# A graph-network kernel: how many gathered tiles are copied on chip instead, and at which rates

## The chip, the cores and the metric

The kernel runs on one core of one Trainium2 chip. The metric is the time of one execution on the device in microseconds (us). A core has five engines, each with its own instruction stream: TensorE (PE in the profile; its weight loads are PEld), VectorE (DVE), ScalarE (ACT), GpSimd (POOL) and SyncE (SP). They wait for one another through semaphores. Transfers are issued from the queues of SP, ACT and POOL.

## The reference, cut to what matters

One layer of message passing on a graph of 12,500 nodes with 64 features and 200,000 edges sorted by destination, 32 features each. All in float32:

```python
msg_in = concatenate([x[src], x[dst], edge_attr], -1)      # 200000 x 160
messages = relu(msg_in @ mW1 + mb1) @ mW2 + mb2
aggregated = segment_sum(messages, dst, 12500)
u = relu(concatenate([x, aggregated], -1) @ uW1 + ub1) @ uW2 + ub2
out = layernorm(x + u)
```

## The kernel before, in words

The edges are cut into 1563 tiles of 128, and six tiles make a group: 261 groups, number 0 to 260. The kernel first multiplies all nodes with the source part of mW1 (table `tab_a` in memory) and with the destination part (`tab_b`). For each group s it then needs, per edge, the row of `tab_a` that belongs to its source, a window of `tab_b` and the edge features.

There are two ways to the source part.

- **Gathered** (`gather`, L209; L220): one indirect transfer per tile, issued by POOL, brings 128 rows of 128 numbers. A group of which all six tiles are gathered costs six. Gathers run ahead of the rest: `rows` has nine buffers, and a gather waits only for the buffer to come free.
- **Copied** (`singly`, L350, and `joined`, L357): in a copied group the last two of the six tiles are not gathered. Instead x stands transposed on chip (`xtop` with zeros below, `xbot` with zeros above), and for each of 128 pairs of edges one column of `xtop` and one of `xbot` are added into a column of a tile `xc`. ACT makes 64 of these columns (an ACTIVATE with a bias, L355), DVE the other 64 (a bitwise or, L362). The addresses are register values that each engine loads in batches (L331). PE then multiplies `xc` with the source part of mW1 (L387), two more products per copied group, four matrix instructions in the profile.

The main loop goes over the groups. In step s, `node_part(s)` lets DVE add the gathered rows to the products of PE (L410, or L407 over four tiles in a copied group), and ACT takes the relu into `h` (L411, or L408). `collect(s-1)` sums `h` of the group before by destination on PE (L443, and counts in L440). `edge_part(s+1)` makes the products of the next group on PE (L384, L387). Between these stand DVE's share of the copies in two or three parts (`joined`), and after them ACT's share in one piece (`singly`). At 32 points of the list, named in `UPD`, the sums are closed (L457, L458) and the nodes up to there are updated and stored (L480 to L533). The intervals between these points are 49 groups at first, 10 in the middle and 3 to 4 at the end. The tile of products `pc` has two buffers, `h` two, and `xc` three.

Which groups are copied, and when their columns are made, is a list worked out ahead of the run. `PACE` gives a rate of copied groups per step from each step on. `progress(s)` is the sum of the rates up to step s. A group s+3 joins the list `COPIED` whenever the sum passes the next whole number, up to group 257 (`FINAL`). `portion` (L318) gives the columns that step s makes: those between `progress(s-1)` and `progress(s)`, in steps of two columns. So a step makes about 64 times the rate on each of the two engines:

```python
PACE = ((11, 0.42), (50, 0.446), (130, 0.429), (261, 0))
FINAL = 258
def progress(s):
    return sum(r * max(0, min(s + 1, b) - a) for (a, r), (b, _) in zip(PACE, PACE[1:]))
COPIED = []
for s in range(NSUB):
    while progress(s) >= len(COPIED) + 1 and s + 3 < FINAL:
        COPIED.append(s + 3)
```

A step makes 26 to 30 of ACT's columns, 28 in most of them, from step 11 to step 253.

Of the kernel before, what the change touches and what calls it, by code (L numbers as in the profile page):

```python
# [70 lines left out]
U8 = mybir.dt.uint8  # L71
YBASE = XBASE + 4 * XCOLS
LEAD = 8
PACE = ((11, 0.42), (50, 0.446), (130, 0.429), (261, 0))
FINAL = 258


def progress(s):

    return sum(r * max(0, min(s + 1, b) - a) for (a, r), (b, _) in zip(PACE, PACE[1:]))  # L80

# [939 lines left out]
```

## Time and profile before

| what | value |
|---|---|
| median of three runs | 1716.34 us (1715.81 to 1716.83) |
| the profiled execution | 1714.18 us, of which the span from first to last instruction is 1712.3 us |
| PE, busy share | 85%, at a mean granted clock of 0.585 |
| ACT, busy share | 90%; 6720 column copies (L355) take 1274.5 us of it |
| DVE, busy share | 62%; 6720 column copies (L362) take 575.0 us, with 442.2 us of idle time ahead of them |
| POOL, busy share | 75%; 1353 gathers of 944 ns each, 0.30 us apart |

The page lists an engine's busy time with the register loads and waits left out. A group of instructions is given as line, engine, operation, tiles, count, then busy time, the mean duration of one, and the idle time of the engine just before it with what ended that. Instructions of ACT and DVE overlap their successor, so the mean duration is longer than the busy time per instruction.

### The profile page before, as it was taken

How to read it: one execution, taken by the hardware profiler on the slowest of the kernel's cores; microseconds unless marked ns; L12 is line 12 of the kernel's file. 1: busy time of each engine (PE TensorE's matmuls, PEld its weight loads, DVE VectorE, ACT ScalarE, POOL GpSimd, SP SyncE). 2: the span in 40 equal slices, each digit the busy share in tenths (PEclk: the TensorE clock that was granted, in tenths of full speed). 3: DMA queues.
4: the chain of work that ended last, by engine and by line, in shares of the span. 5: the costliest groups of instructions: out<-in, count | busy, mean ns of one | idle time of the engine just before them, and what ended most of it. 6: DMA issues, size and time to landing. Idle time of an engine off the chain costs nothing. (4 is left out here: it accounts for less than half of the span.)

```text
span 1712.3 us, 46949 instructions
## 1 busy us (share of the span) xinstructions
PE 1456.2 (85%) x9604; PEld 1251.9 (73%) x9604; DVE 1053.3 (62%) x7476; ACT 1537.2 (90%) x7151; POOL 1279.5 (75%) x1362
## 2 busy tenths in 40 slices
PE   2696889897888888898889999898878898999998
PEld 2585778776777786887777777776667677777776
DVE  1426666666666666666666666666666666666662
ACT  0277999999999999999999999999999999999982
POOL 7777777777777777777777777777777777777774
PEclk8675555555555555555555555556665656565666
DMA  8783434433333333333334343333333333443342
GB/s 209 207 180 100 119 109 127 117 104 89 98 93 101 95 100 97 99 103 100 104 101 110 106 113 103 106 110 103 106 103 109 111 107 108 113 112 105 105 113 76
DMA packets 205949, 191.23 MB, mean 112 GB/s; under 512 B 56129, under 2 KB 172053, under 8 KB 205669
## 3 DMA queue, kind: packets, MB, share of 16 engines
q1 hardware_dynamic: 147828, 92.48, 19.6%
q0 software_dynamic: 43296, 86.79, 18.6%
q10 hardware_dynamic: 14546, 8.93, 1.9%
q8 instruction: 91, 1.49, 0.4%
q14 instruction: 188, 1.54, 0.3%
HBM read 170.55 MB, written 17.50 MB: 110 GB/s over the span
## 5 line engine op out<-in xcount | busy, mean ns | idle before, releaser
L220 POOL DMA_INDIRECT xg<-tab_a,src_s x1293 | 1221.1, 944 | 394.2 <-issue 357.6
L355 ACT ACTIVATE xc<-xtop,xbot 128x1 f32 x6720 | 1274.5, 288 | 32.9 <-issue 22.9
L362 DVE TENSOR_TENSOR xc<-xtop,xbot 128x1 int32 x6720 | 575.0, 154 | 442.2 <-issue 429.5
L443 PE MATMUL sums<-sel,h 128*128 128x32 f32 x3126 | 643.3, 373 | 83.0 <-ACT h L408 42.5
L443 PEld LDWEIGHTS sums<-sel,h 128*128 128x128 f32 x3126 | 609.5, 296 | 108.0 <-ACT h L408 48.2
L384 PE MATMUL pc<-rhs,l 64*128 64x128 f32 x3126 | 418.7, 413 | 59.3 <-DMA l<-in_eT 15.2
L384 PEld LDWEIGHTS pc<-rhs,l 64*128 64x128 f32 x3126 | 348.8, 293 | 119.4 <-issue 62.8
L410 DVE TENSOR_TENSOR h<-pc,xg 128x768 f32<-128x768 f32 x147 | 139.5, 949 | 57.5 <-PE pc L384 27.8
L411 ACT ACTIVATE h<-h 128x768 f32<-128x768 f32 x147 | 122.3, 833 | 27.6 <-DVE h L410 26.8
L254 DVE TENSOR_TENSOR l<-l,cps 128x768 f32<-128x768 int32 (+1 forms) x134 | 126.7, 946 | 29.3 <-DMA l<-in_dst_row 17.4
L440 PEld LDWEIGHTS <-one 128*1 128x1 bf16 x1563 | 56.9, 83 | 89.3 <-issue 80.3
L440 PE MATMUL cnt<-sel,one 128*1 128x32 bf16 x1563 | 92.6, 187 | 0.5 <-issue 0.3
L408 ACT ACTIVATE h<-pc 128x768 f32<-128x768 f32 x105 | 83.8, 798 | 7.8 <-DVE pc L407 7.4
L407 DVE TENSOR_TENSOR pc<-pc,xg 128x512 f32<-128x512 f32 x105 | 73.4, 699 | 27.9 <-PE pc L387 23.8
L387 PE MATMUL pc<-w1a,xc 64*128 64x128 f32 x420 | 81.2, 388 | 0.0
L260 DVE TENSOR_TENSOR sel<-cps,drc 128x384 f32<-128x384 f32 x131 | 71.4, 545 | 12.0 <-PE sums L443 12.0
L387 PEld LDWEIGHTS pc<-w1a,xc 64*128 64x128 f32 x420 | 72.1, 301 | 0.0
L220 POOL DMA_INDIRECT xg<-in_x,src_s x60 | 57.4, 957 | 19.1 <-issue 17.7
L494 PE MATMUL cps<-ux,xw 128*128 128x64 f32 x252 | 45.9, 341 | 20.0 <-DVE sel L260 17.4
L480 PE MATMUL pu<-xw,uz 128*128 128x480 f32 (+1 forms) x64 | 61.2, 1059 | 0.0
L598 ACT COPY tb<-pb 128x512 f32<-128x512 f32 (+1 forms) x13 | 7.4, 570 | 58.7 <-DMA tab_a<-tb 26.8
L494 PEld LDWEIGHTS cps<-ux,xw 128*128 128x128 f32 x252 | 41.1, 247 | 25.4 <-DVE sel L260 19.6
(105 smaller groups left out, 691.6 us busy)
## 6 DMA issues: line engine op xcount, KB each, us to landing
l<-in_dst_row SPq DMA_DIRECT2D x262, 96.0 KB
l<-in_eT SPq DMA_DIRECT2D x262, 96.0 KB
xg<-tab_a,src_s POOLq DMA_INDIRECT x1293
rhs<-tab_b SPq DMA_DIRECT2D x361, 32.0 KB
tab_b<-tb SPq DMA_DIRECT2D x13, 512.0 KB
rhs<-tab_b SPq DMA_DIRECT2D x387, 16.0 KB
tab_a<-tb ACTq DMA_DIRECT2D x12, 512.0 KB
out<-y SPq DMA_DIRECT2D x31, 128.0 KB
```

Source lines behind the costliest of these rows:

```text
L220: nc.gpsimd.indirect_dma_start(out=a[:, i, :] if s < XG else a[:, i // 2, i % 2, :], out_offset=None, in_=A[:, :] if s >= XG else x[:, :], ...
L254: nc.vector.tensor_tensor(l[r], l[r].bitcast(I32), node[r].unsqueeze(2).broadcast_to([r.stop - r.start, SUP // 2, P]), op=ALU.is_equal)
L355: nc.scalar.activation(o[:, e:e + 1], top.bitcast(F32), AF.Identity, bias=bot.bitcast(F32))
L362: nc.vector.tensor_tensor(o[:, e:e + 1].bitcast(I32), top.bitcast(I32), bot.bitcast(I32), op=ALU.bitwise_or)
L384: nc.tensor.matmul(pc[:, b, k, :], L[g][q:q + 64, m, :], rhs[g % 2][q:q + 64, w, :], start=s >= XG or k == 0, stop=s >= XG and not copied)
L387: nc.tensor.matmul(pc[:, b, k, :], xc[s][q:q + 64], w1a[q:q + 64], start=False, stop=True)
L408: nc.scalar.activation(h, pc, AF.Relu)
L410: nc.vector.tensor_tensor(h[:, b, :m], pc[:, b, :m], a[:, b, :m], op=ALU.add)
L411: nc.scalar.activation(h[:, b, :m], h[:, b, :m], AF.Relu)
L440: nc.tensor.matmul(pn[:, bass.ds(ws[i], WIN)], one, SB[g][:, k0 + i, :, 1], start=False, stop=ends and i == n - 1)
L443: nc.tensor.matmul(ps[:, bass.ds(ws[i], WIN)], h[:, i % 2, i // 2, :], S[g][:, k0 + i, :], start=False, stop=ends and i == n - 1)
L494: nc.tensor.matmul(py[:, i], xw[u % 2][:, i * P:(i + 1) * P], ux, start=i == 0, stop=False)
```

## The change

Only the list is changed: the three rates of `PACE` are higher. The list `COPIED` has 108 groups instead of 105. The first is group 16 as before, the last 257 instead of 256. From the third on most entries stand one to six groups earlier than the entry of the same rank before.

```diff
-PACE = ((11, 0.42), (50, 0.446), (130, 0.429), (261, 0))
+PACE = ((11, 0.435), (50, 0.4565), (130, 0.438), (261, 0))
 FINAL = 258
```

Worked out with `progress` and `portion`, the columns that ACT makes (DVE makes the same number):

| steps | rate | columns before | columns after |
|---|---|---|---|
| 11 to 49 | 0.42 to 0.435 | 1048 | 1084 |
| 50 to 156 | 0.446 to 0.4565, from 130 on 0.429 to 0.438 | 3024 | 3094 |
| 157 to 252 | 0.429 to 0.438 | 2636 | 2692 |
| 253 and 254 | 0.429 to 0.438 | 12 | 42 |
| all | | 6720 | 6912 |

Three copied groups more also mean six gathers fewer on POOL (1347 instead of 1353), twelve matrix instructions more (L387), and three times L407 with L408 in place of L410 with L411.

## The prediction

> **What bounds the kernel now.** Two engines could set the pace, and they are the two between which the change shifts work: POOL gets six gathers fewer, ACT gets 192 column copies more. So I first ask of each whether it ever waits. POOL on the page:
>
> ```profile
> POOL 7777777777777777777777777777777777777774
> ...
> L220 POOL DMA_INDIRECT xg<-tab_a,src_s x1293 | 1221.1, 944 | 394.2 <-issue 357.6
> ```
>
> POOL shows 7 in every slice, but this is POOL at its peak: 944 ns of gather and 0.30 us of issue ahead of each, 1.2495 us from start to start, without a break from 2.8 us to the last one that begins at 1692.5 us. ACT is busy for 90% of the span. Both look full, so the page can't decide, and I go to the busy times in five stretches. I cut them at the starts of the relu of groups 10, 50, 157 and 253, read from the timeline; the last four are shown. The columns behind the length are PE, PEld, DVE, ACT, POOL (busy us and count), the clock and the transfers:
>
> ```profile
> 121.00:375.00 254.00, 211.96 (x1450) 193.49 (x1450) 170.31 (x1177) 230.27 (x1090) 192.12 (x204) 0.53 0.41 113
> 375.00:1036.00 661.00, 574.66 (x3657) 500.59 (x3656) 432.40 (x3275) 655.68 (x3174) 499.78 (x530) 0.55 0.36 100
> 1036.00:1660.00 624.00, 551.52 (x3519) 456.62 (x3518) 398.72 (x2904) 595.09 (x2807) 471.58 (x500) 0.60 0.39 108
> 1660.00:1712.00 52.00, 44.05 (x308) 35.80 (x307) 16.50 (x43) 14.29 (x35) 25.47 (x27) 0.72 0.30 84
> ```
>
> From 375 to 1036 us ACT is busy for 655.7 of 661 us: it has 5.3 us to spare in 107 groups, and is the bound. From 1036 to 1660 us it is idle for 28.9 of 624 us, 0.30 us in a group. POOL's lead tells the rest. By the timeline, from the end of a group's last gather to DVE's add of its rows are 36 us for group 24, about 25 for group 50, 13 for group 130 and 2.3 for group 157, where the data have only just landed. So ACT and the others, slower at first by their late start, catch up with POOL at about group 157. From there on the lead goes between 2.2 and 10 us, and is 9.4 us at group 253.
>
> How ACT sets the pace is seen step by step in its timeline (start, us, then the instructions that follow one another without a gap):
>
> ```profile
> 630.69 0.86 ACT L411 ACTIVATE h<-h 128x768 f32<-128x768 f32 x1
> 631.42 5.32 ACT L355 ACTIVATE xc<-xtop,xbot 128x1 f32 x28
> 636.61 0.83 ACT L408 ACTIVATE h<-pc 128x768 f32<-128x768 f32 x1
> 637.30 5.32 ACT L355 ACTIVATE xc<-xtop,xbot 128x1 f32 x28
> 642.49 0.87 ACT L411 ACTIVATE h<-h 128x768 f32<-128x768 f32 x1
> 643.23 5.70 ACT L355 ACTIVATE xc<-xtop,xbot 128x1 f32 x30
> 648.79 0.83 ACT L408 ACTIVATE h<-pc 128x768 f32<-128x768 f32 x1
> ```
>
> A step from relu to relu takes 5.92 and 5.88 us with 28 copies, and 6.30 with 30. Two copies are 0.38 us, **one copy is 0.187 to 0.19 us** of the step's time, with nothing beside it. Of the 107 steps from 50 to 156 nearly all lie on such a level, moved only by the instructions of an update.
>
> Whom DVE's adds wait for from 1036 to 1660 us (total, times, longest):
>
> ```profile
> DVE h L410 <- PE pc L384: 18.6, 14, 2.4
> DVE pc L407 <- PE pc L387: 15.6, 9, 2.8
> ...
> DVE h L410 <- DMA xg<-tab_a,src_s: 4.0, 6, 0.9
> ```
>
> DVE waits 34.2 us for PE's products and 4.0 us for gathered rows. ACT's idle time in this stretch is mostly the shadow of PE, which comes late at updates (there it waits for DVE's copy of the counts, L457, up to 3.7 us) and its granted clock is 0.60 on average there, 0.55 in the stretch before. POOL's share is small.
>
> **The change, part by part.** *Six gathers fewer*: 6 x 1.2495 = 7.5 us off POOL's chain, so its last gather begins at 1685.0 instead of 1692.5. This helps only where somebody waits for rows: 1.7 + 0.3 us from 375 to 1036, 4.0 us from 1036 to 1660, and 7.0 us at the end (groups 258 and 259). In the first two stretches most of these waits of DVE leave ACT's relu without any gap; I count 1 us.
>
> *192 copies more on ACT*, by stretch and at 0.187 us:
>
> - Steps 11 to 49: 36 copies, 6.7 us. ACT's idle time there is 23.7 us, but 8.0 of it is one wait for a weight and 6.7 one wait for DVE; some 9 us are left, spread over the steps. In the steps that have none the copies cost all, in the others part. Step by step (what exceeds the step's own idle time) this gives **+4.0 us**.
> - Steps 50 to 156: 70 copies, 13.1 us, against 5.3 us of idle time that lies in a few steps. Step by step **+12.6 us**.
> - Steps 157 to 252: 56 copies, 10.5 us. They cost nothing if all the 28.9 us of idle time can take them, and 10.5 us if none can. The idle time lies in bits of 0.2 to 0.6 us and in a few of 1 to 2.9 us at updates; a step that goes from 26 to 28 copies needs 0.37 us. About half of these steps have it: **+5.0 us**.
> - Steps 253 and 254: 12 copies become 42. Step 253 had 12 copies and took 3.4 us; with 28 it is a full step of about 6.2 us, +2.8 us. The 14 of step 254 take 2.6 us, of the 2.92 us that ACT waits there for DVE; but DVE's 14 columns (2 us) stand ahead of the add that it waits for. I take +1.5 us.
>
> *192 columns more on DVE*: 575.0 us / 6720 = 86 ns each, 16.4 us. The register loads come in batches of up to four pairs of columns, so more columns per batch add few: the built program has three more on DVE (1039 instead of 1036). ACT covers it: the add of one group ended at 562.28 and ACT began its relu at 563.21, because it was still copying. DVE is about 1 us ahead there; without this cover it would be the same 0.1 us per group that ACT pays, so it is not added.
>
> *Twelve more matrix instructions* (81.2 / 420 = 0.19 us, 2.3 us in all) lie beside ACT's copies; three adds of 699 instead of 949 ns and relus of 798 instead of 839 ns give back 0.9 us. I set the two against each other.
>
> *Buffers of the gathers*: with ACT later and POOL earlier, the lead grows by some 30 us towards the end. A gather begins 41 to 49 us after its buffer came free in the last hundred groups, and 11 us at the tightest place, group 24, where the delay is still below 3 us. So POOL keeps running.
>
> *The tail* (1660 to 1712 us): PE is busy for 44 of 52 us and bounds most of it. The two waits for rows, of groups 258 and 259:
>
> ```profile
> 1683.88 0.96 DVE L410 TENSOR_TENSOR h<-pc,xg 128x768 f32<-128x768 f32 x1 [2.27 <-DMA xg<-tab_a,src_s]
> ...
> 1692.96 0.96 DVE L410 TENSOR_TENSOR h<-pc,xg 128x768 f32<-128x768 f32 x1 [4.77 <-DMA xg<-tab_a,src_s]
> ...
> 1693.97 0.71 PE L384 MATMUL pc<-rhs,l 64*128 64x128 f32 x6 [0.48 <-DVE h L410]
> ...
> 1695.77 1.10 PE L494 MATMUL cps<-ux,xw 128*128 128x64 f32 x8 [1.09 <-DVE y L526]
> ```
>
> While DVE waits here, PE works on; what PE loses by it is 0.48 + 1.09 us. So the late rows give back 1.6 us, with 0.2 more of the first wait: **-1.8 us**, between 0 and the full 7.0. What is late next is PE's chain of updates.
>
> **The sum**: 4.0 + 12.6 + 5.0 + 2.8 + 1.5 - 1.8 - 1.0 = +23.1 us. I round to +22, since the late steps lean on idle time of PE's that shifts from run to run. On the profiled execution 1714.2 + 22 = 1736 us; that run lies 2.2 us below the median of the three, so **1738 us** on the median's footing. Bounds: if every copy is paid in full and nothing comes back, 192 x 0.187 = +36 us, 1752. If the first stretch costs nothing and the third absorbs all, 12.6 - 1 + 0 to 2.5 = +12 to +14 us, 1729.
>
> A rule speaks against this. POOL's gathers leave no gap but their issue from 2.8 to 1692.5 us (the row above). The Trainium skill, in "Perfetto Trace Analysis", section 'What "DMA-bound" means', counts a kernel as bound on the DMA sequencer when the issuing engine's track is solid with DMA slices. By it the sum would be rival A's alone. The trace disagrees between group 24 and 157, where the rows lie landed for up to 36 us before they are used.
>
> **The rivals.** *A, POOL is the bound* (faster): then the end follows the last gather, and 7.5 us go: 1716.3 - 7.5 = 1709. For it: DVE waits for rows at groups 258 and 259, and the lead is down to 2.2 us at 157 and again at 231 to 236. It decides only if the groups arrive at 253 as early as POOL lets them. But ACT alone forbids it: group 157 comes 16.6 us later, and its own work then takes 595.1 + 10.5 us without any idle time, so group 253 comes at 1036 + 16.6 + 605.6 = 1658.2 at the best, against 1660.1 now. Chance 0.04.
>
> *B, the third stretch gives all back* (same): ACT's idle time there was all a shadow of POOL's pace, and goes once POOL is far ahead. Then group 253 comes at 1658.2, 1.9 us earlier than before, and with +2.5 of the tail the time is 1716 to 1717. Against it: the 34.2 us that DVE waits for PE, with the rows in place. Chance 0.05.
>
> *C, all is paid*: DVE and PE bind in the same steps as ACT, idle time absorbs nothing: +32 to +36 us, 1748 to 1752. Chance 0.13. The forecast has 0.78.
>
> That the change does nothing is no rival here: the built program has the 192 ACTIVATEs more.
>
> A measurement of this kernel can tell some 0.2%, 3.4 us, from no change. Faster: A and one hundredth of the forecast's 0.78, whose terms are estimates, 0.05. Same: B, 0.05. Slower: the rest of the forecast and C, 0.90. The range 1722 to 1752 takes in the bounds of the unknown terms and C.
>
> **What would show it.** Right: steps of 28 copies still take 5.9 us and only their mix changes; ACT's idle time from group 50 to 157 stays under 6 us; group 157 comes 15 to 18 us later with a lead of about 25 us; DVE waits for no rows after group 150; the last gather begins near 1685. Wrong: ACT's idle time from 157 to 253 falls to near zero (B), or POOL still binds at the end (A).

## The result, and the profile after

The changed kernel takes **1726.8 us** (median of six runs, 1724.1 to 1736.8), the kernel before 1716.6 us (1715.8 to 1717.9). The ratio is 1.0069, 95% interval 1.0044 to 1.0094: slower by 10.2 us, where 22 were forecast. The profiled execution is the fastest of the six, 1724.1 us with a span of 1722.3.

Ten of the twelve experiments below ran on chips where the kernel before itself takes 2474 to 2491 us, and are told apart from the two at 1715 us.

POOL and ACT in the whole span, changed kernel:

```profile
POOL 7777777777777777777777777777777777777771
...
L220 POOL DMA_INDIRECT xg<-tab_a,src_s x1287 | 1215.9, 945 | 392.4 <-issue 367.7
L355 ACT ACTIVATE xc<-xtop,xbot 128x1 f32 x6912 | 1309.4, 288 | 24.5 <-issue 16.8
```

POOL again runs without a break. Its last gather begins at 1685.7 us; 1685.0 was computed. ACT's copies are busy for 34.9 us more, 0.182 us for each of the 192. The stretches, cut again at the relus of groups 10, 50, 157 and 253 (same columns as before: PE, PEld, DVE, ACT, POOL, clock, transfers):

```profile
123.70:383.90 260.20, 217.41 (x1451) 198.38 (x1447) 172.62 (x1216) 237.87 (x1128) 196.81 (x209) 0.50 0.42 112
383.90:1055.60 671.70, 575.58 (x3662) 500.19 (x3661) 437.99 (x3348) 667.67 (x3242) 507.93 (x538) 0.55 0.37 100
1055.60:1673.20 617.60, 542.72 (x3524) 447.96 (x3523) 401.45 (x2952) 601.44 (x2864) 466.74 (x495) 0.61 0.41 108
1673.20:1722.30 49.10, 42.41 (x307) 34.21 (x306) 18.95 (x72) 19.84 (x65) 10.36 (x11) 0.76 0.26 68
```

Groups 50 to 157 take 671.7 us instead of 661, with ACT idle for 4.0 of them. Groups 157 to 253 take **617.6 instead of 624.1 us**, although ACT is busy 6.3 us longer there. ACT's idle time fell from 28.9 to 16.2 us. So up to group 157 the change costs time, and behind it a part comes back. Step by step ACT looks as before; a step of 30 copies takes 6.29 and 6.26 us from relu to relu, one of 28 takes 5.92:

```profile
642.60 0.86 ACT L411 ACTIVATE h<-h 128x768 f32<-128x768 f32 x1
643.34 5.68 ACT L355 ACTIVATE xc<-xtop,xbot 128x1 f32 x30
648.89 0.82 ACT L408 ACTIVATE h<-pc 128x768 f32<-128x768 f32 x1
649.58 5.70 ACT L355 ACTIVATE xc<-xtop,xbot 128x1 f32 x30
655.15 0.87 ACT L411 ACTIVATE h<-h 128x768 f32<-128x768 f32 x1
655.88 5.32 ACT L355 ACTIVATE xc<-xtop,xbot 128x1 f32 x28
661.07 0.83 ACT L408 ACTIVATE h<-pc 128x768 f32<-128x768 f32 x1
```

Whom DVE's adds wait for from group 157 to 253 (total, times, longest):

```profile
DVE pc L407 <- PE pc L387: 9.8, 7, 2.3
...
DVE h L410 <- PE pc L384: 7.3, 9, 1.2
...
DVE h L410 <- DMA xg<-tab_a,src_s: 2.8, 3, 2.1
```

The waits for PE were 34.2 us before and are 17.1 now (18.7 with a wait of L407 for L384), although the change gives PE a few products more and none less. The waits for rows have hardly moved, 4.0 to 2.8 us, though POOL's lead is now 20 us and more. Here the name is wrong: by the trace of the transfers (32 packets of POOL's queue for each gather), the rows of every group in this stretch had landed at least 18.8 us before their add. Read by the names, PE would have become faster. What did change is the lead: from a group's last gather to its add are 25.6 us at group 157 (2.3 before), 21.8 at 185, 29.3 at 253. The experiments ask whether that was the cause.

### The profile page after: what moved, and what is told of

It reads as the page before. It is cut to its first block, busy times and chain, and to the rows that moved or that the text cites. A ratio compares the mean times of both kernels' runs of the same rounds, so it can differ in the third digit from the quotient of the medians.

```text
span 1722.3 us, 47370 instructions
## 1 busy us (share of the span) xinstructions
PE 1452.1 (84%) x9616; PEld 1245.9 (72%) x9616; DVE 1067.6 (62%) x7668; ACT 1568.4 (91%) x7343; POOL 1274.4 (74%) x1356
## 3 DMA queue, kind: packets, MB, share of 16 engines
q1 hardware_dynamic: 147828, 92.48, 19.6%
## 4 chain that ended last, share of the span: by engine, by line
ACT 44%; POOL 12%; issue 10%; DVE 10%; PE 8%; ACTq 7%; DMA 7%; DVEq 2%; SPq 1%; POOLq 0%
ACT xc L355 37%; POOL xg L220 12%; ACTq L331 7%; DVE xc L362 4%; ACT h L411 3%; PE sums L443 3%; DMA xg<-tab_a,src_s 3%; ACT h L408 2%; PE pc L384 2%; DVEq L331 2%; DVE l L254 1%; DVE h L410 1%; DMA tab_a<-tb 1%; DMA l<-in_dst_row 1%; DMA l<-in_eT 1%
## 5 line engine op out<-in xcount | busy, mean ns | idle before, releaser
L355 ACT ACTIVATE xc<-xtop,xbot 128x1 f32 x6912 | 1309.4, 288 | 24.5 <-issue 16.8
L362 DVE TENSOR_TENSOR xc<-xtop,xbot 128x1 int32 x6912 | 590.4, 155 | 463.9 <-issue 451.7
L384 PE MATMUL pc<-rhs,l 64*128 64x128 f32 x3126 | 420.7, 412 | 71.3 <-DVE tb L606 22.2
L384 PEld LDWEIGHTS pc<-rhs,l 64*128 64x128 f32 x3126 | 349.9, 290 | 132.9 <-issue 61.4
L410 DVE TENSOR_TENSOR h<-pc,xg 128x768 f32<-128x768 f32 x144 | 136.6, 949 | 37.4 <-PE pc L384 18.0
L411 ACT ACTIVATE h<-h 128x768 f32<-128x768 f32 x144 | 119.7, 832 | 19.5 <-DVE h L410 18.9
L408 ACT ACTIVATE h<-pc 128x768 f32<-128x768 f32 x108 | 86.2, 798 | 4.6 <-DVE pc L407 4.5
L407 DVE TENSOR_TENSOR pc<-pc,xg 128x512 f32<-128x512 f32 x108 | 75.5, 699 | 22.3 <-PE pc L387 15.7
L387 PE MATMUL pc<-w1a,xc 64*128 64x128 f32 x432 | 83.2, 384 | 0.0
L260 DVE TENSOR_TENSOR sel<-cps,drc 128x384 f32<-128x384 f32 x131 | 71.5, 546 | 10.2 <-PE sums L443 10.1
L387 PEld LDWEIGHTS pc<-w1a,xc 64*128 64x128 f32 x432 | 74.1, 299 | 0.0
L494 PE MATMUL cps<-ux,xw 128*128 128x64 f32 x252 | 43.4, 327 | 12.0 <-DVE sel L260 10.2
L481 PE MATMUL pu<-sums_s,w2u 128*128 128x480 f32 (+1 forms) x64 | 53.4, 936 | 0.0
```

Source lines behind the costliest of these rows:

```text
L355: nc.scalar.activation(o[:, e:e + 1], top.bitcast(F32), AF.Identity, bias=bot.bitcast(F32))
L362: nc.vector.tensor_tensor(o[:, e:e + 1].bitcast(I32), top.bitcast(I32), bot.bitcast(I32), op=ALU.bitwise_or)
L384: nc.tensor.matmul(pc[:, b, k, :], L[g][q:q + 64, m, :], rhs[g % 2][q:q + 64, w, :], start=s >= XG or k == 0, stop=s >= XG and not copied)
L387: nc.tensor.matmul(pc[:, b, k, :], xc[s][q:q + 64], w1a[q:q + 64], start=False, stop=True)
L408: nc.scalar.activation(h, pc, AF.Relu)
L410: nc.vector.tensor_tensor(h[:, b, :m], pc[:, b, :m], a[:, b, :m], op=ALU.add)
```

## The experiments

Two theories stand against each other. **Lead**: with POOL's lead near zero the other engines were held to POOL's pace from group 157 on, also where the waits name PE. **Work**, the prediction's: the idle time there comes from PE at the updates, whatever the lead. A third, **clock**, is that PE was granted more clock by chance.

**Kernel before, 16 gathers off POOL.** It changes the lead and nothing on ACT or DVE. SyncE's queue fills these 16 tiles with other rows, so this kernel's result is another. The last of them belongs to group 152, so from group 157 on only the lead differs (`...` stands for lines left out):

```diff
+    PLAIN = range(62, 157, 6)
 ...
         for i, t in enumerate(gathered_tiles(s)):
+            if s in PLAIN and i == 0:
+                nc.sync.dma_start(a[:, 0, 0, :], A[t * 8 % 8192:t * 8 % 8192 + P, :])
+                continue
             nc.gpsimd.indirect_dma_start(
```

> The kernel before, with 16 gathers less on POOL: the first tile of 16 groups (62, 68, ... 152) is filled by a plain transfer of 128 consecutive rows from SyncE's queue, so these tiles hold other rows than the reference's. Run again because the chip of the first run took some 2480 us for the kernel before, with all engines waiting on their instruction streams; what is asked is the behaviour at 1716 us. Lead theory (a thin lead of POOL held the other engines up from group 157 on, also where the waits name PE): the stretch from the relu of group 157 to that of 253 falls from 624.1 to 607 us, within 4, and the whole time is 1695 to 1703 us. Work theory (the idle time comes from PE at the updates, whatever the lead): the stretch stays at 624 us within 4, the whole time is 1711 to 1715. Clock theory (PE's granted clock, by chance): 612 to 624 us for the stretch, going with the clock.

Measured: **1701.5 us** against 1714.6 of the kernel before on the same chip, ratio 0.9927 (0.9906 to 0.9949). Up to group 157 it goes as before (1036.3 against 1036.0 us), with a lead of 19.5 us. The stretch from 157 to 253 takes 610.7 us: within the lead theory's range (603 to 611), at a granted clock between 0.60 and 0.66 in its parts. I cut it at groups 185, 195 and 235. First the kernel before, then this one:

```profile
1036.00:1217.60 181.60, 158.22 (x1009) 134.89 (x1008) 115.00 (x842) 171.87 (x813) 137.24 (x146) 0.58 0.38 107
1217.60:1283.60 66.00, 54.27 (x364) 43.92 (x365) 41.19 (x304) 62.26 (x294) 50.00 (x53) 0.63 0.37 104
1283.60:1537.60 254.00, 225.15 (x1462) 185.88 (x1459) 166.53 (x1218) 247.12 (x1169) 191.83 (x204) 0.61 0.39 109
1537.60:1660.10 122.50, 113.98 (x693) 92.03 (x691) 76.02 (x543) 113.84 (x533) 92.57 (x99) 0.59 0.39 108
```

```profile
1036.30:1209.30 173.00, 150.98 (x991) 126.62 (x991) 114.46 (x834) 170.34 (x814) 130.64 (x140) 0.60 0.41 109
1209.30:1274.50 65.20, 53.95 (x382) 43.50 (x380) 41.01 (x303) 61.95 (x293) 49.36 (x53) 0.66 0.39 104
1274.50:1528.30 253.80, 228.28 (x1455) 188.07 (x1452) 166.28 (x1212) 247.02 (x1170) 191.89 (x204) 0.60 0.41 109
1528.30:1647.00 118.70, 110.53 (x683) 88.91 (x682) 76.43 (x550) 113.51 (x534) 89.73 (x96) 0.60 0.41 110
```

Of the 13.4 us gained, 8.6 sit in the first row, the 28 groups from 157 to 185. There the kernel before is at **POOL's pace**. These groups have 144 gathers, 144 x 1.2495 = 179.9 us, and the lead goes from 2.3 to 4.1 us: 179.9 + 1.8 = 181.7, measured 181.6. This sum alone proves nothing, since an add comes one lead after its last gather at any lead. What shows the bound is the comparison: with the rows ahead the same groups need 173.0 us, and ACT idles for 2.7 us of them instead of 9.7. The packets agree. In the kernel before, 12 of these 28 adds began within 1.35 us of the end of their rows' last packet, as did the five whose waits are named for rows (0.8 to 1.35 us); from 195 to 235 it is 5 adds of 40, and with 16 gathers fewer the smallest distance is 12.4 us from 157 to 185.

From 195 to 235 both take the same time: the groups' own pace is 6.35 us there, POOL's 206 gathers make 6.43 a group, and a lead of 7.9 us lasts for forty groups. The last row gains 3.8 us, and why isn't told apart: with the early part alone, below, the rows are ahead there too and it gains 1.0.

DVE's waits for PE fall with the lead, though the edit does nothing to PE. From group 157 to 185, first the kernel before, then this one, whose line numbers are four higher:

```profile
DVE h L410 <- PE pc L384: 5.8, 3, 2.4
DVE pc L407 <- PE pc L387: 4.0, 2, 2.5
```

```profile
DVE h L414 <- PE pc L388: 2.1, 1, 2.1
...
DVE pc L411 <- PE pc L391: 1.5, 2, 0.8
```

ACT's copies are alike in both kernels. The clock is 0.58 and 0.60 in the first row, and that hardly explains it: PE is busy for 87% of the stretch in both, and for 87% from group 50 to 157 as well, where its clock was only 0.55 and ACT idled for 5.3 us in 661.

**Only the early part of the change, and less of it:**

```diff
-PACE = ((11, 0.42), (50, 0.446), (130, 0.429), (261, 0))
+PACE = ((11, 0.435), (50, 0.448), (130, 0.429), (261, 0))
```

> Only the early part of the change, and less of it: rates 0.435 from step 11, 0.448 from step 50, 0.429 from step 130 as before; 106 copied groups. 0.745 of a copied group more are made up to group 157, 48 columns on ACT, and none in the rate after. Lead theory: group 157 comes 7.5 us later (0.157 us a column, as the changed kernel had it for steps 50 to 156) with a lead of 10 to 12 us; the stretch from 157 to 253 is 611 to 614 us, as in the kernel with fewer gathers, since the lead stays over 4 us until near the end; the whole time is 1706 to 1711 us, faster than both kernels. Work theory: the stretch stays at 624 us, the whole time is 1722 to 1725 us, slower than before.

Measured: 1719.8 us against 1714.5, ratio 1.0032 (1.0013 to 1.0051): slightly slower. Both theories miss. The time lies 9 us above the lead theory's and 2 below that of the work theory, and the stretch from 157 to 253 takes 616.5 us, where the one said 611 to 614 and the other 624. Its parts:

```profile
1048.20:1221.70 173.50, 153.45 (x1005) 128.58 (x1005) 114.88 (x842) 170.16 (x814) 131.19 (x139) 0.61 0.41 109
1221.70:1286.00 64.30, 52.04 (x371) 42.09 (x371) 41.16 (x302) 62.00 (x293) 48.70 (x52) 0.69 0.39 105
1286.00:1543.20 257.20, 228.77 (x1446) 187.93 (x1444) 165.66 (x1217) 247.83 (x1170) 194.39 (x207) 0.59 0.41 108
1543.20:1664.70 121.50, 114.32 (x706) 92.09 (x705) 75.99 (x547) 113.41 (x534) 91.93 (x98) 0.60 0.41 109
```

The mechanism shows again: 173.5 us from 157 to 185, with a lead of 15 to 9 us and the copies of the kernel before. What failed is the lead theory's account around it. Group 157 comes 12.2 us later, not 7.5: 1.9 us of that stand at group 10 already, ahead of any change, and the 32 columns more from group 16 to 50 cost 7.3 us. The last two parts take 257.2 and 121.5 us, 3.4 and 2.8 more than with 16 gathers fewer, at equal copies and with a lead of 6.9 us at the least. So this list buys 8 us and pays 10.

**Runs on the other chips.** There the kernel before takes 2474 to 2491 us. What the engines wait for there is seen in a kernel with the changed rates up to step 156:

```profile
DVE xc L362 <- issue: 701.4, 1157, 2.2
POOL xg L220 <- DVE h L410: 435.5, 112, 14.4
...
ACT xc L355 <- issue: 356.4, 580, 1.8
```

ACT pauses for 356 us amid its copies, where the kernel before paused for 23 at 1715 us, and POOL waits for buffers: its lead is 68 to 86 us from group 157 on, as far as nine buffers allow. The profile names no cause for these pauses; that the engines wait for their instruction streams, as an expectation above has it, isn't shown. None of the theories' numbers applies, so these runs decide nothing between them. Their ratios to the kernel before on the same chip:

The 16 gathers taken off POOL, first run:

> The kernel before, with 16 gathers less on POOL: the first tile of 16 groups (62, 68, ... 152) is filled by a plain transfer of 128 consecutive rows from SyncE's queue, so these tiles hold other rows than the reference's. POOL's lead at group 157 is about 22 us instead of 2.3, with the copies of the kernel before. Lead theory: the stretch from group 157 to 253 falls from 624.1 to 607 us, within 4 (617.6 of the changed kernel less 56 copies of 0.187), the end gets 2 to 5 us shorter as well, and the whole time is 1695 to 1703 us. Work theory: the stretch stays at 624 us within 4, the whole time is 1711 to 1715. Clock theory: 612 to 624 us for the stretch, going with the granted clock.

Measured 0.9935 (0.9900 to 0.9971). POOL cannot have been the bound there, since it waits for buffers; why fewer gathers help all the same is open.

The changed kernel with 18 gathers more into a spare tile, twice:

```diff
+    EXTRA = range(62, 152, 5)
 ...
+        if s in EXTRA:
+            nc.gpsimd.indirect_dma_start(
+                out=spare_rows[s % 2], out_offset=None, in_=A[:, :],
+                in_offset=bass.IndirectOffsetOnAxis(ap=src_s[:, s:s + 1], axis=0))
         xg[s] = buf, a
```

> The changed kernel with 18 gathers more on POOL, into a tile that nobody reads, one each at groups 62 to 147: POOL falls back by 18 x 1.25 = 22.5 us, so its lead at group 157 is about 3 us instead of 25.6, with the same copies on ACT and DVE. Read from the stretch between the relu of group 157 and that of group 253 (before 624.1 us, changed kernel 617.6 us). Lead theory (a thin lead of POOL held the other engines up from group 157 on, also where the waits name PE): the stretch grows to 624 to 632 us. Work theory (as predicted: the idle time there comes from PE at the updates, whatever the lead): 617 us, within 4. Clock theory (the changed kernel's PE was granted a little more clock by chance): 612 to 624 us, going with the clock and not with the lead. For all three the whole time is at least the last gather at 1708 plus some 20 us: 1728 us or more.

> The changed kernel with 18 gathers more on POOL, into a tile that nobody reads, one each at groups 62 to 147; run again for the same reason as the other second run. POOL falls back by 18 x 1.25 = 22.5 us, so its lead at group 157 is about 3 us instead of 25.6, with the copies of the changed kernel. Lead theory: the stretch from group 157 to 253 goes from 617.6 to 624 us or more (up to 632), slow where the lead is under some 4 us. Work theory: 617 us within 4. For both the end follows the last gather, at 1685.7 + 22.5 = 1708, by some 20 us: 1728 us or more for the whole.

Measured 1.0055 (1.0027 to 1.0083) and 1.0069 (1.0033 to 1.0105). The counter-test of the lead, taking it away from the changed kernel, was thus not made at 1715 us.

The changed rates up to step 156 and 0.429 after (`(130, 0.438), (157, 0.429)` in `PACE`), twice:

> The changed rates up to step 156, the rate of before (0.429) from step 157 on: 107 copied groups. The lead at group 157 is the 25.6 us of the changed kernel. Lead theory: the stretch from 157 to 253 is 607 to 611 us, the whole time 1715 to 1719. Work theory: the stretch is that of the kernel before, 624 us, and the whole time 1730 to 1734. Clock theory: between these, and spread from run to run.

> The changed rates up to step 156, the rate of before (0.429) from step 157 on: 107 copied groups; run again for the same reason. The lead at group 157 is the 25.6 us of the changed kernel. Lead theory: the stretch from 157 to 253 is that of the kernel with fewer gathers, 610.7 us within 3; group 157 comes 19 us later than before, and the whole time is 1717 to 1722. Work theory: the stretch is that of the kernel before, 624 us, and the whole time 1730 to 1734.

Measured 1.0044 (1.0014 to 1.0074) and 1.0011 (0.9977 to 1.0045).

Half of the change in each part (`PACE = ((11, 0.4275), (50, 0.4513), (130, 0.4335), (261, 0))`):

> Half of the change in each part of the list: rates 0.4275, 0.4513 and 0.4335, 106 copied groups. Lead at group 157 about 13 us. Lead theory: half of the copies are paid up to group 157 (+9 us), but the stretch from 157 to 253 falls to about 612 us, and the end is shorter by 3: about 1712 us, faster than the kernel before. Work theory: half of everything, +11 us over before less the little that rows give back, 1724 to 1728. Clock theory: as work theory, with a spread of 5 us.

Measured 0.9973 (0.9937 to 1.0009), no difference that can be told. It was not run at 1715 us.

The early part alone, two runs:

> Only the early part of the change, and less of it: rates 0.435 from step 11, 0.448 from step 50, 0.429 from step 130 as before; 106 copied groups. 0.745 of a copied group more are made up to group 157, 48 columns on ACT, and none in the rate after. Lead theory: group 157 comes 7.5 us later (0.157 us a column, as the changed kernel had it for steps 50 to 156) with a lead of 10 to 12 us; the stretch from 157 to 253 is 611 to 614 us, as in the kernel with fewer gathers, since the lead stays over 4 us until near the end; the whole time is 1706 to 1711 us, faster than both kernels. Work theory: the stretch stays at 624 us, the whole time is 1722 to 1725 us, slower than before.

> Only the early part of the change, and less of it: rates 0.435 from step 11, 0.448 from step 50, 0.429 from step 130 as before; 106 copied groups; run again because the kernel before took 2491 us on the chip of the first run. 0.745 of a copied group more are made up to group 157, 48 columns on ACT, and none in the rate after. Lead theory: group 157 comes 7.5 us later (0.157 us a column, as the changed kernel had it for steps 50 to 156) with a lead of 10 to 12 us; the stretch from 157 to 253 is 611 to 614 us, as in the kernel with fewer gathers, since the lead stays over 4 us until near the end; the whole time is 1706 to 1711 us, faster than both kernels. Work theory: the stretch stays at 624 us, the whole time is 1722 to 1725 us, slower than before.

Measured 1.0001 (0.9969 to 1.0032) and 0.9963 (0.9931 to 0.9996).

The changed kernel with 62 columns of a copied pair on ACT and 66 on DVE (`ACTS, CHUNK = 62, 8`), twice:

> The changed kernel with 62 of a copied pair's 128 columns on ACT and 66 on DVE, instead of 64 each: 216 columns move from ACT to DVE. It asks who pays for a copied group. If ACT alone sets the pace of the steps (the prediction, which took DVE to be covered), ACT's chain is 216 x 0.187 = 40 us shorter; then POOL becomes the bound again, with its last gather at 1685.7 and some 20 us behind it: 1706 to 1712 us, faster than both kernels. If DVE stands just behind ACT (its columns take 0.15 us of its stream each, with the register loads, and its waits for others are some 0.2 us a group), it takes over: 1720 to 1732 us, like the changed kernel or a little slower, ACT then waiting for DVE's adds.

> The changed kernel with 62 of a copied pair's 128 columns on ACT and 66 on DVE, instead of 64 each: 216 columns move from ACT to DVE; run again because the kernel before took 2476 us on the chip of the first run. It asks who pays for a copied group. If ACT alone sets the pace of the steps (the prediction, which took DVE to be covered), ACT's chain is 216 x 0.187 = 40 us shorter; then POOL becomes the bound again, with its last gather at 1685.7 and some 20 us behind it: 1706 to 1712 us, faster than both kernels. If DVE stands just behind ACT (its columns take 0.15 us of its stream each, with the register loads, and its waits for others are some 0.2 us a group), it takes over: 1720 to 1732 us, like the changed kernel or a little slower, ACT then waiting for DVE's adds.

Measured 0.9962 (0.9919 to 1.0006) and 0.9945 (0.9922 to 0.9969). Whether this list with fewer columns on ACT beats both kernels at 1715 us stays open; the changed kernel was not run on these chips, so the part that the moved columns have in it is not told apart either.

## Why the prediction was right or wrong

By the profiled executions, in us of the span:

| part | forecast | measured |
|---|---|---|
| up to group 16 | 0 | +1.2 |
| groups 16 to 50 (forecast from step 11 on) | +4.0 | +7.4 |
| groups 50 to 157 | +12.6 | +11.0 |
| groups 157 to 253 (the 1.0 for rows counts from group 50) | +5.0 - 1.0 | -6.5 |
| from 253 to the end | +2.8 + 1.5 - 1.8 | -3.1 |
| sum | +23.1 | +10.0 |

The +1.2 us is no effect of the change: the changed kernel is 3.0 us later at group 10 already, ahead of its first additional copy, and gains 1.7 of that back up to group 16.

*ACT is the bound early*: right. ACT's idle time from 50 to 157 is 4.0 us (under 6 was forecast), and the lead at group 157 is 25.6 (about 25). Group 157 comes 19.6 us later, a little more than the 15 to 18 forecast. The 70 columns cost 0.157 us each, where 12.6 / 70 = 0.18 was forecast.

*Idle time takes a part of the first copies*: wrong. From group 16 to 50 the 32 columns cost 7.4 us, 0.23 each, in the changed kernel and 7.3 with the early part alone. Both stretches, before and after:

```profile
169.30:375.30 206.00, 176.77 (x1210) 162.21 (x1210) 139.85 (x1001) 198.08 (x950) 155.70 (x166) 0.53 0.41 115
```

```profile
170.50:383.90 213.40, 183.52 (x1214) 168.41 (x1214) 142.84 (x1034) 204.32 (x981) 161.29 (x172) 0.50 0.42 113
```

ACT's busy time grows by 6.2 us and its idle time by 1.2, from 7.9 to 9.1: nothing was absorbed. The kernel before with 16 gathers fewer, which is the same up to here, takes 206.0 us too, so spread between runs is an unlikely reason. Why a column costs more than ACT's 0.187 us here is open.

*"POOL's share is small"* from 157 to 253, the term of -1.0 us: **this step failed**, and most of the miss is in it. Rows in time are worth 8.1 to 8.6 us in the groups from 157 to 185 alone (two kernels with the copies of before), where the prediction went by the name of the wait and by a mean over 96 groups. The trace held a sign: a lead that stays between 1.7 and 6.8 us over 28 groups, under 5 in 25 of them, so that the groups keep step with POOL. (The prediction gave 2.2 us as the least.) It is a sign only, for the lead is as small around group 235, where the groups go at their own pace. With late rows every add came late by a little, and what DVE then waited for was the next engine in the ring (DVE's add, ACT's relu, PE's sums and next products, DVE's next add): PE, that had been late from the step before. That chain from late rows to PE is argued; that the waits for PE go with the lead is shown, from 9.8 us (5.8 + 4.0) between 157 and 185 to 3.6 (2.1 + 1.5) with 16 gathers fewer. Over the whole stretch they go from 34.2 to 20.3 us there and to 24.3 with the early part alone, so the greater part of them was PE's own, as the prediction had it.

So rival B had the right mechanism for 28 of the 96 groups, and 0.05 was little for it. It fails where it took all idle time for POOL's shadow: 16.2 us are left with a lead of 20 us and more.

*The price of 56 columns from 157 to 253*, forecast +5.0: +6.9 against the kernel with 16 gathers fewer, +1.1 against the early part alone, which has the copies of before and a lead of 6.9 us and more. From 157 to 185, where the new list makes 18 columns more, it is 175.4 against 173.0 and 173.5. The runs differ by 3 to 4 us in the later parts at equal copies, so the size is between 1 and 7 and no closer.

*Rival A*: its bound held. Group 253 could not come earlier than ACT's own work allowed, and came at 1673.2. The rule of the Trainium skill ("Perfetto Trace Analysis", section 'What "DMA-bound" means'), by which a solid track of the issuing engine marks a kernel as bound on its DMA sequencer, does not fit the kernel as a whole. It fits 28 groups of the kernel before: the trace agrees with it there, 181.6 us at 179.9 us of gathers, and 173.0 with the rows ahead. It has to be read with the lead beside it.

*The tail*: +2.5 was forecast, -3.1 measured. Step 253 cost +3.0 as computed (+2.8), step 254 only 0.1 instead of 1.5. The gain after them isn't explained. Rows in time alone don't give it: with 16 gathers fewer, and rows 10 us ahead, the tail takes 52.6 us, with the early part alone 53.9, before 52.2. PE is busy for most of it, and its busy time goes with the granted clock: 42.4 us at 0.76 in the changed kernel, 44.1 at 0.72 before, 44.6 at 0.69 with the early part alone, 47.1 at 0.66 with 16 gathers fewer. So clock may be part of the reason; one profile of each can't show it.

The direction was right and the time lies in the range, but the size was not: 10.2 us where 22 were forecast. That the range holds it is in part luck. The lowest bound that the prediction worked out for its own terms was 1729 us, the measured time lies below it, and no term led down to 1722.

## What to carry to other kernels

Where a producer runs ahead, read its lead group by group and compare the consumer's advance with the producer's own pace over each stretch, before believing the names of the waits. A stretch that keeps the producer's pace at a small lead may be bound by it, whoever is named; taking a few of the producer's items away ahead of the stretch shows whether it is. A mean of idle time over a long stretch hides a short one that is bound by something else. A trade between two engines that are both full gains little: here 64 columns cost ACT 10 to 15 us and save POOL 2.5. It can pay only where the lead is used up; even the list with more copies ahead of that place alone bought 8 us and paid 10.

## What the runs showed of the hardware that was not expected

The changed kernel spreads more from run to run, 1724.1 to 1736.8 us in six runs, and the early part alone 1715.2 to 1726.5 in eight. The kernel before goes from 1715.8 to 1717.9 in six runs, and from 1711.0 to 1717.8 in eleven on another chip. What widens the spread isn't known.

In ten of the twelve experiments, on five chips, the kernel before took 1.44 to 1.45 times its time (2474 to 2491 us). The kernels profiled there show gaps of "issue" amid ACT's and DVE's copies, and gathers of the same 945 ns. What these chips lack isn't settled by the profiles.
